# Probability rows of 16 or of 8 keys a head in the pooled attention of a two-layer kernel

## The chip, the cores and the metric

The kernel runs on one core of one Trainium2 chip. The metric is the device time of one execution in microseconds (us); the time before is the median of three runs, 1923.88 us (1922.08 to 1924.26). In what follows PE is TensorE, PEld its weight loads, DVE VectorE, ACT ScalarE, POOL GpSimd and SP SyncE; "L1619" is line 1619 of the kernel before.

## The reference

Two layers over 2048 tokens of width 512. The first is an RWKV recurrence beside a gated feed-forward of two experts. The second is attention over pooled keys beside a mixture of 16 routed experts (each token uses 4) and 2 shared ones. The change lies in the second layer's attention. There are 16 heads, 4 key groups, and at this length the first 1792 tokens are pooled in blocks of 64, so that they make 28 keys; the last 256 tokens are keys of their own:

```python
pool = lambda a: jnp.concatenate([a[:, :, :remote].reshape(Bq, HKV, nblk, MB, a.shape[-1]).mean(axis=3), a[:, :, remote:]], axis=2)
k_sem2, k_geo2, v2 = (pool(k_sem), pool(k_geo), pool(v))
k_pos = jnp.concatenate([jnp.arange(nblk) * MB + (MB - 1), jnp.arange(remote, Tq)])
...
scores = jnp.einsum('bhqd,bhkd->bhqk', q_sem, k_sem2) * (1.0 / jnp.sqrt(float(DS))) + jnp.einsum('bhqd,bhkd->bhqk', q_geo, k_geo2) * (1.0 / jnp.sqrt(float(DG)))
scores = scores * jnp.exp(logit_scale)[None, :, None, None]
mask = k_pos[None, :] <= pos[:, None]
scores = jnp.where(mask[None, None], scores, NEG_INF)
probs = jax.nn.softmax(scores, axis=-1)
out = jnp.einsum('bhqk,bhkd->bhqd', probs, v2)
out = out.transpose(0, 2, 1, 3).reshape(Bq, Tq, H * DV)
return out @ Wo
```

A key is seen by the queries at or behind its position. A tile of 128 tokens with number i therefore sees at most 2 (i + 1) pooled keys: 4 in tile 1, 8 in tile 3, 28 in tile 13. (Token tile 0 holds queries that see no key at all and gets a treatment of its own.)

## The kernel before

All work is in 32-bit floats. A scheduler places every instruction on its engine's queue by priorities and dependencies; the written order is only its starting point. Each engine then works through its queue in order.

The first layer takes the trace up to about 975 us. The second layer then makes the routing, keys and values (up to about 1200 us), the two last token tiles with their unpooled keys (`full_group`, L1443 to L1500), the shared experts (`hidden_shared`, `down_shared`, up to 1333 us), and then one long stage in which two things are interleaved by hand:

- **Row tiles.** Tokens were sorted by expert into tiles of 128 rows; 64 tiles always exist, up to 80 may, and 73 do here. Row tile j loads its rows (`x`, L1674) and its expert's weights (`w`, L674 to L678) on SP, turns the rows on PE (`tp`, L1681), multiplies (`ph`, L1688), and a tile later multiplies back (`py`, L1712). DVE scales the result into `y` (L1717, four buffers), and POOL adds its two halves into `comb` in memory by two indirect DMAs with addition (L1720). Each of them waits for the one before it in the same half. Tiles from number 65 on are under a condition, one branch each (L1737), and the scheduler moves nothing across these branches. Weights have three buffers, rows of x four.
- **Attention pieces.** After most of the first 64 row tiles one piece of `attention()` (L1630) is taken: the queries of two token tiles (`pq`, L1367; DVE's rotation by cos and sin, L1378 to L1383), the scores of one token tile (`scores`, L1571: `ps` on PE at L1576 and L1582, DVE's L1592 adds the mask and leaves the result in a buffer, then the softmax), or probabilities and values of one token tile (`turned` and `values`).

`turned` (L1598) brings a token tile's probabilities, kept as heads by keys, to keys on partitions: `pt` by transposes on PE (L1608), `sT` by a copy on ACT (L1613). `values` (L1616) multiplies each 128 rows of sT with the matching rows of values already multiplied by Wo (`pw`, L1619), and ACT copies the result into xT (L1623). How many of each a token tile needs follows from the room its probabilities stand in (`room_of`, L1564):

- tile 0: 32 keys a head, 512 columns: four transposes and four products;
- tiles 1 to 7: one of three buffers `near` of 16 keys a head, 256 columns: two and two. Only the first 2 (i + 1) keys of a head are written, and the rest was zeroed once at L1562;
- tiles 8 to 13: a buffer `wide` each, 32 keys a head: four and four.

The rows of values for 32 keys are `vo`; for 16 keys a copy in another order, `vo8`, is put together through memory: SP writes vo out (L1530) and reads it back in 16 pieces of 16 rows (L1531 to L1537). Tiles 0 to 4 go through `turned` and `values` inside the stage, tiles 5 to 13 (`LAST`) after its last row tile, while the last scatters into comb land. Then SP loads comb back (L1764), and ACT, DVE and SP finish and store the output (`close`, L1770 to L1780).

The xo loads (L1750) fetch, from row tile 48 on in the written order, what `close` adds at the end.

Of the kernel before, what the change touches and what calls it, by code (L numbers as in the profile page):

```python
# [9 lines left out]
F32 = mybir.dt.float32  # L10
# [7 lines left out]
P = 128  # L18
T = 2048
D = 512  # L20
# [24 lines left out]
H = 16  # L45
# [3 lines left out]
MB = 64  # L49
# [3 lines left out]
KP = 32  # L53
# [4 lines left out]
NARROW = 16  # L58
# [19 lines left out]
def tile_kernel(ctx: ExitStack, tc: tile.TileContext, a: dict):  # L78
    nc = tc.nc
# [4 lines left out]
    ident = const.tile([P, P], F32, name="ident")  # L84
# [30 lines left out]
    vo_d = dram.tile([P, HKV, D], F32, name="vo_d")  # L115
# [235 lines left out]
    for i in range(0, NT, 2):  # L351
        xin = n0.tile([P, 2, D], F32, tag="xin", bufs=NT // 2, name="xin")
        nc.sync.dma_start(
            out=xin, in_=a["x"][i * P : (i + 2) * P, :].rearrange("(n p) d -> p n d", p=P)
# [10 lines left out]
        out=wdc, in0=gate0_w[:, :, 1], in1=gate0_w[:, :, 0], op=ALU.subtract  # L365
    )
    wdp = n0ps.tile([P, NC, P], F32, tag="tp", name="wdp")
    for c in range(NC):
        dg = n0.tile([P, P], F32, tag="dg", bufs=2, name="dg")
        nc.vector.tensor_scalar(  # L370
            out=dg, in0=ident, scalar1=wdc[:, c : c + 1], scalar2=None, op0=ALU.mult
# [16 lines left out]
        out=upper, in_=upper, compare_op=ALU.is_gt, fill=0.0, base=0,  # L388
# [7 lines left out]
        out=eno, in0=col[:, 0:NST], scalar1=float(P), scalar2=None, op0=ALU.mult  # L396
# [4 lines left out]
    for i in range(0, NT, 2):  # L401
# [4 lines left out]
            out=shift, in0=mv[:, :, 0], scalar=-1.0, in1=rstd, op0=ALU.mult, op1=ALU.mult  # L406
        )
        for j in range(2):
# [6 lines left out]
                out=junk, in0=xn, in1=wdiff, scale=1.0, scalar=0.0, op0=ALU.mult, op1=ALU.add,  # L415
# [13 lines left out]
    for _ in range(2):  # L429
# [3 lines left out]
        out=sel[:, :, 0], in0=dl, scalar1=0.0, scalar2=None, op0=ALU.is_le  # L433
# [3 lines left out]
        out=sel[:, :, 1], in0=dl, scalar1=0.0, scalar2=None, op0=ALU.is_gt  # L437
# [3 lines left out]
        out=m, in0=dl, scalar=-1.0, in1=dl, op0=ALU.mult, op1=ALU.min  # L441
# [8 lines left out]
    for o, tri in ((0, upper), (N2, sums)):  # L450
        nc.tensor.matmul(
            out=tab[:, o : o + N2], lhsT=tri, rhs=sel.rearrange("p n e -> p (n e)"),
# [7 lines left out]
        out=run.rearrange("p e n -> p (e n)"), data0=newrow.rearrange("p e n -> p (e n)"),  # L460
# [8 lines left out]
        out=full, in0=own.to_broadcast([P, NT // 2]), in1=eno2[:, :, 1], op=ALU.is_gt  # L469
# [4 lines left out]
        out=paired[:, 0:1], in0=paired[:, 1:2], scalar1=2.0 * P, scalar2=None, op0=ALU.mult  # L474
    )
    nc.vector.tensor_tensor(
        out=pair_e[:, 0 : NSP - 1], in0=eno2[0:1, :, 0],
# [3 lines left out]
        out=pair_e[:, NSP - 1 : NSP], in0=own[0:1, :], in1=paired[0:1, 0:1], op=ALU.is_le  # L481
    )
    nc.vector.tensor_scalar(
        out=paired[:, 1:2], in0=paired[:, 0:1], scalar1=-1.0, scalar2=float(T),
# [4 lines left out]
        out=run[:, 1, :], in0=run[:, 1, :], scalar1=paired[:, 0:1], scalar2=None, op0=ALU.add  # L489
# [3 lines left out]
        out=row, in0=within, in1=run.rearrange("p e n -> p n e"), op=ALU.add  # L493
# [3 lines left out]
        out=alone, in0=row[:, :, 0], scalar1=paired[:, 0:1], scalar2=paired[:, 1:2],  # L497
# [10 lines left out]
        out=past, in0=bc(rowf, 2, C3), in1=bc(eno, 1, C3), op=ALU.is_ge  # L508
# [6 lines left out]
        out=place, in0=at, scalar=float(-P), in1=rowf, op0=ALU.mult, op1=ALU.add  # L515
    )
    nc.vector.tensor_tensor(
        out=past, in0=bc(at, 2, C3), in1=bc(col[:, 0:NST], 1, C3), op=ALU.is_equal
# [4 lines left out]
    for f in range(3):  # L523
        nc.vector.tensor_tensor(
            out=put[:, :, f, :], in0=past, in1=bc(facts[:, f, :], 2, C3), op=ALU.mult
# [3 lines left out]
    for i0 in range(0, NT, HN):  # L529
        if i0 == 2 * HN:  # L530
# [3 lines left out]
            out=hot, in0=bc(place[:, i0 : i0 + HN], 2, [P, HN, P]),  # L534
            in1=bc(col, 1, [P, HN, P]), op=ALU.is_equal,
        )
        for i in range(HN):
            nc.tensor.matmul(
                out=listed, lhsT=hot[:, i, :], rhs=put[:, i0 + i],
# [194 lines left out]
    for b in range(BEFORE):  # L734
# [14 lines left out]
    vo = ak.tile([P, HKV, D], F32, name="vo")  # L749
# [33 lines left out]
        out=m_pool, in_=m_pool, compare_op=ALU.is_ge, fill=0.0, base=1 - MB,  # L783
# [3 lines left out]
        out=n_pool, in_=n_pool, compare_op=ALU.is_ge, fill=MASKED, base=1 - MB,  # L787
# [15 lines left out]
    for t_ in n_full:  # L803
        own = t_[:, t_.shape[1] - P :]
        nc.gpsimd.affine_select(
            out=own, in_=own, compare_op=ALU.is_ge, fill=MASKED, base=0,
# [39 lines left out]
    for i in range(NT):  # L846
        yg = tr.tile([P, D], F32, tag="yg", bufs=6, name="yg")
        nc.gpsimd.indirect_dma_start(
            out=yg, out_offset=None, in_=ys0,
            in_offset=bass.IndirectOffsetOnAxis(ap=slot0[:, i : i + 1], axis=0),  # L850
        )
        g = acc[:, i, 0:D]
# [5 lines left out]
    for b in range(BEFORE, NRB):  # L858
        for i, po in carried(b):
            g = acc[:, i, 0:D]  # L860
# [3 lines left out]
    for b in range(NRB):  # L864
# [4 lines left out]
        for s in range(n):  # L869
            nc.vector.tensor_tensor(  # L870
                out=xr[:, s, :], in0=xr[:, s, :], in1=acc[:, i0 + s, 0:D], op=ALU.add
# [3 lines left out]
        for s in range(n):  # L875
            i = i0 + s
            nc.vector.tensor_scalar(
                out=acc[:, i, 0:D], in0=xr[:, s, :], scalar1=mv[:, s, 0:1],
# [3 lines left out]
        if (i + 1) % (TB // P) == 0:  # L882
            t0 = i + 1 - TB // P
            pl = m1y.tile([NR, TB], F32, tag="py", name="pl")
            for c in range(NC):
                nc.tensor.matmul(  # L886
                    out=pl, lhsT=cent[:, c, :], rhs=xT[:, c, t0 * P : (i + 1) * P],
# [10 lines left out]
    for b in range(NRB):  # L898
        rows2 = slice(b * RB, (b + 1) * RB)
        if b < PER:  # L900
            k0 = b * RB // MB
            nc.vector.tensor_reduce(
                out=xsum[:, :, k0 : k0 + RB // MB],
                in_=xT[:, :, rows2].rearrange("p c (n m) -> p c n m", m=MB),
                axis=AX.X, op=ALU.add,
            )
        else:
            nc.vector.tensor_reduce(
                out=xsum[:, :, NBLK : NBLK + 1],
                in_=xT[:, :, rows2].rearrange("p c (n m) -> p c n m", m=LW),  # L910
# [23 lines left out]
        out=upper, in_=upper, compare_op=ALU.is_gt, fill=0.0, base=0,  # L934
# [52 lines left out]
    with tc.tile_pool(name="rt", bufs=1, side="right") as rt, tc.tile_pool(  # L987
        name="rt2", bufs=2, side="right"
# [9 lines left out]
        for dst, tri in ((within, upper), (count, sums)):  # L998
            nc.tensor.matmul(
                out=dst.rearrange("p n e -> p (n e)"), lhsT=tri,  # L1000
# [6 lines left out]
            out=run.rearrange("p e n -> p (e n)"), data0=newrow.rearrange("p e n -> p (e n)"),  # L1007
# [5 lines left out]
            out=full, in0=run[:, :, NT - 1 : NT].to_broadcast([P, NR, NT]),  # L1013
# [6 lines left out]
            out=end, data0=sums[:, 0:NR], data1=ntl, initial=0.0, op0=ALU.mult, op1=ALU.add  # L1020
# [7 lines left out]
            out=run, in0=bc(first_tile, 2, [P, NR, NT]), scalar=float(P), in1=run,  # L1028
# [4 lines left out]
            out=row, in0=within, in1=run.rearrange("p e n -> p n e"), op=ALU.add  # L1033
# [3 lines left out]
        for k in range(KR):  # L1037
            one = rt2.tile([P, NT, NR], F32, tag="one", bufs=1, name="one")
            nc.vector.scalar_tensor_tensor(
                out=one, in0=rank, scalar=float(k + 1), in1=row, op0=ALU.is_equal, op1=ALU.mult,  # L1040
# [10 lines left out]
            out=acc[:, :, D : D + NR], in0=row, in1=bc(tot, 2, [P, NT, NR]), op=ALU.mult  # L1051
# [5 lines left out]
        for i in range(NT):  # L1057
            for k in range(KR):
                ins = nc.gpsimd.indirect_dma_start(  # L1059
                    out=xs,  # L1060
                    out_offset=bass.IndirectOffsetOnAxis(ap=slot[:, i, k : k + 1], axis=0),
                    in_=acc[:, i, :], in_offset=None,
# [21 lines left out]
        for m0 in (0, HM):  # L1084
# [4 lines left out]
                out=past, in0=bc(tno[:, ms], 2, sh3), in1=bc(end, 1, sh3), op=ALU.is_ge  # L1089
# [419 lines left out]

    sem = wq.tile([P, NC, H, KP], F32, name="sem")  # L1510

    vo8 = wq.tile([P, 2, D], F32, name="vo8")
    with tc.tile_pool(name="fold", bufs=1, side="right") as fold:
        wqs = fold.tile([P, NC, H * DH], F32, name="wqs")
        nc.sync.dma_start(out=wqs, in_=a["Wq_sem"])
# [12 lines left out]
                )  # L1528
            nc.scalar.copy(sem[:, :, 4 * g : 4 * g + 4, :], pa)
    nc.sync.dma_start(out=vo_d, in_=vo)  # L1530
    for p in range(2):  # L1531
        for u in range(2):
            for j in range(4):
                nc.sync.dma_start(
                    out=vo8[(4 * u + j) * NARROW : (4 * u + j + 1) * NARROW, p, :],
                    in_=vo_d[j * KP : j * KP + NARROW, 2 * p + u, :],
                )  # L1537

    down_shared(NTB - 1, hT)
    for tb in range(NTB - 1):  # L1540
# [17 lines left out]
    WIDE = NARROW * MB // P  # L1558
# [5 lines left out]
    def room_of(i):  # L1564

        if i == 0:
            return aq.tile([P, H, KP], F32, tag="t1", name="all_keys"), KP
        nk = (i + 1) * P // MB
        return (near[i % 3] if i < WIDE else wide[i - WIDE]), nk

    def scores(i, qg, u):  # L1571
        cols = slice(u * P, (u + 1) * P)
# [25 lines left out]
    def turned(i):  # L1598

        s = waiting.pop(i)  # L1600
        keys = s.shape[2]
        each = P // keys
        nw = H // each

        pool, tag = (m1y, "py") if i in LAST else (aps, "pa")
        pt = pool.tile([P, nw, P], F32, tag=tag, name="pt")
        for g in range(nw):
            nc.tensor.transpose(  # L1608
                pt[:, g, :], s[:, each * g : each * (g + 1), :].rearrange("p h k -> p (h k)"),
                ident,  # L1610
            )
        sT = aq2.tile([P, HKV, P], F32, tag="sT", name="sT")
        nc.scalar.copy(sT[:, 0:nw, :], pt)  # L1613
        return i, nw, sT, vo if keys == KP else vo8

    def values(i, nw, sT, by_row):  # L1616
        pw = aps.tile([P, NC, P], F32, tag="pa", name="pw")
# [274 lines left out]
```

## Time and profile before

| what | value |
|---|---|
| median of three runs | 1923.88 us (1922.08 to 1924.26) |
| the profiled execution | 1919.63 us |
| its span, first to last instruction | 1917.9 us |
| mean granted PE clock | 0.990 |
| PE busy over the span | 1848.1 us (96%) |
| PEld, DVE, ACT, POOL busy | 1286.8, 762.0, 536.5, 461.5 us |
| DMA | 381.40 MB, mean 199 GB/s |
| stage of row tiles | 1334 us to about 1876 us |
| transposes pt L1608 from near | 14, of which 6 before 1500 us |
| products pw L1619 | 84 records from 1330 us on, two for each product of 128x512 |

The table of windows gives, for a stretch of time, each engine's busy time, the granted clock in parts of one, and the mean busy share of the 16 DMA engines. The chain that ended last is followed back from the last instruction: each piece has its start, its length and what ran. A line of the timeline has start, length, engine, source line, operation, what it writes and reads, and in brackets how long the engine was idle before and what ended that.

### The profile page before, as it was taken

What the parts mean: (1) busy time and instruction counts of PE and PEld (TensorE: products, weight loads), DVE (VectorE), ACT (ScalarE), POOL (GpSimd) and SP (SyncE); (2) the same over time, 40 slices, a digit from 0 to 9 for tenths busy, and PEclk for the clock granted to TensorE, in tenths of its full rate; (3) what the DMA queues carried; (4) which work ended last, traced back from release to release, by engine and by line L of the source; (5) the groups of instructions that cost most, each with busy time, mean ns of one, the idle gap of its engine ahead of it and who ended that gap; (6) DMA issues with size and microseconds to landing.
All of it is one profiled execution on the core that took longest, in us unless ns stands there. A gap on an engine that the chain in (4) does not pass through costs nothing.

```text
span 1917.9 us, 23670 instructions
## 1 busy us (share of the span) xinstructions
PE 1848.1 (96%) x8107; PEld 1286.8 (67%) x8107; DVE 762.0 (40%) x1528; ACT 536.5 (28%) x1006; POOL 461.5 (24%) x349
## 2 busy tenths in 40 slices
PE   6999999999999999999989999999999999999996
PEld 4777777777877777777533654445767777777662
DVE  8354545272725435352166543421323223233313
ACT  6224232332423232332134112221222222222223
POOL 0211121120212111010210453000344444444341
PEclk9899999999999999999999999999999999999998
DMA  8657686635563434437461553122999999999896
GB/s 269 223 180 249 234 272 213 211 99 173 163 222 113 154 120 133 143 99 252 149 213 49 180 207 115 50 83 71 316 298 306 329 309 269 279 272 269 229 257 186
DMA packets 235989, 381.40 MB, mean 199 GB/s; under 512 B 19405, under 2 KB 136909, under 8 KB 234969
## 3 DMA queue, kind: packets, MB, share of 16 engines
q1 hardware_dynamic: 205784, 332.79, 52.3%
q0 software_dynamic: 28784, 45.63, 10.6%
q10 hardware_dynamic: 1296, 1.41, 0.3%
q8 instruction: 67, 1.10, 0.2%
q14 instruction: 58, 0.47, 0.1%
HBM read 294.04 MB, written 85.72 MB: 198 GB/s over the span
## 4 chain that ended last, share of the span: by engine, by line
PE 56%; DMA 6%; DVE 1%; issue 1%; ACT 1%; POOL 1%; SPq 0%; DVEq 0%; ACTq 0%; POOLq 0%
PE ph L1688 10%; PE py L1712 9%; PE pg L585 8%; PE py L607 4%; PE py L1121 4%; PE ph L972 3%; DMA comb<-y,to 3%; PE pq L1367 2%; PE proj L219 2%; PE po L727 2%; PE tp L1681 2%; PE ps L1576 1%; PE ps L1582 1%; PE pl L886 1%; PE pw L1492 1%
## 5 line engine op out<-in xcount | busy, mean ns | idle before, releaser
L585 PE MATMUL pg<-xg,w 128*128 128x256 f32 (+1 forms) x2304 | 494.9, 368 | 0.0
L585 PEld LDWEIGHTS pg<-xg,w 128*128 128x128 f32 x2304 | 419.5, 190 | 90.5 <-issue 42.3
L1720 POOL DMA_INDIRECT comb<-y,to x146 | 228.1, 1562 | 313.9 <-DMA comb<-y,to 183.4
L607 PE MATMUL py<-wd,hT 128*128 128x512 f32 x544 | 257.1, 593 | 3.5 <-DVE hT L592 3.5
L1688 PEld LDWEIGHTS ph<-xg,w 128*128 128x128 f32 (+1 forms) x1776 | 202.0, 182 | 40.4 <-ACT xg L1683 36.6
L1688 PE MATMUL ph<-xg,w 128*128 128x128 f32 (+1 forms) x1776 | 216.3, 278 | 0.7 <-issue 0.3
L592 DVE TENSOR_TENSOR hT<-sg,pg 128x256 f32<-128x256 f32 (+1 forms) x144 | 57.3, 402 | 380.4 <-ACT sg L590 380.2
L1712 PE MATMUL py<-w,ht 128*128 128x512 f32 (+1 forms) x438 | 207.8, 593 | 0.0
L590 ACT ACTIVATE sg<-pg 128x256 f32<-128x256 f32 (+1 forms) x144 | 53.0, 370 | 359.6 <-PE pg L585 359.3
L607 PEld LDWEIGHTS py<-wd,hT 128*128 128x128 f32 x544 | 102.2, 190 | 73.0 <-issue 61.9
L1717 DVE TENSOR_SCALAR y<-py,g 128x512 f32<-128x512 f32 x73 | 54.6, 748 | 219.7 <-PE py L1712 219.7
L958 ACT ACTIVATE ht<-ph,b1t 128x128 f32<-128x128 f32 (+1 forms) x222 | 81.2, 366 | 178.2 <-PE ph L1688 176.1
L1712 PEld LDWEIGHTS py<-w,ht 128*128 128x128 f32 (+1 forms) x438 | 75.9, 191 | 51.4 <-issue 45.2
L1683 ACT COPY xg<-tp 128x512 f32<-128x512 f32 x74 | 43.3, 585 | 186.9 <-PE tp L1681 186.9
L1121 PE MATMUL py<-w,hT 128*128 128x512 f32 (+1 forms) x192 | 89.4, 595 | 0.0
L972 PE MATMUL ph<-xT,w 128*128 128x512 f32 (+1 forms) x192 | 88.0, 597 | 0.0
L1059 POOL DMA_INDIRECT xs<-acc,slot x64 | 63.2, 987 | 66.0 <-DMA xs<-acc,slot 43.6
L267 POOL TENSOR_TENSOR ex<-st_p,qt 128x1024 f32<-128x1024 f32 x8 | 18.3, 2287 | 235.7 <-DVE qt L266 235.7
L727 PE MATMUL po<-wo,yb 128*128 128x512 f32 x128 | 57.4, 607 | 9.7 <-ACT acc L736 9.7
L1681 PEld LDWEIGHTS tp<-ident,x 128*128 128x128 f32 x296 | 36.9, 140 | 38.6 <-issue 20.8
L219 PE MATMUL proj<-xm,wr 128*128 128x256 f32 x256 | 61.5, 396 | 0.0
L219 PE MATMUL proj<-xm,wk 128*128 128x256 f32 x256 | 60.2, 389 | 0.0
(412 smaller groups left out, 2142.5 us busy)
## 6 DMA issues: line engine op xcount, KB each, us to landing
w<-in_w_dram SPq DMA_DIRECT2D x152, 352.0 KB
w<-in_w_dram SPq DMA_DIRECT2D x152, 256.0 KB
w<-in_w_gate_dram SPq DMA_DIRECT2D x72, 512.0 KB
w<-in_w_up_dram SPq DMA_DIRECT2D x72, 512.0 KB
wd<-in_w_down_dram SPq DMA_DIRECT2D x72, 512.0 KB
xs<-zero SPq DMA_DIRECT2D x16, 1360.0 KB
x<-xs SPq DMA_DIRECT2D x74, 272.0 KB
w<-in_w_dram SPq DMA_DIRECT2D x76, 192.0 KB
```

Of the source, the lines that this page charges most:

```text
L219: nc.tensor.matmul(out=ps[:, j, :], lhsT=w_[:, c, (o0 + j) * P : (o0 + j + 1) * P], rhs=xm[:, c, :], start=(c == 0), stop=(c == NC - 1),)
L585: nc.tensor.matmul(out=pg[:, i, 0:n], lhsT=w[:, c, i * FH + f * P : i * FH + (f + 1) * P], rhs=xg[:, c, 0:n], start=(c == 0), stop=(c == N ...
L607: nc.tensor.matmul(out=p, lhsT=hT[:, u * P : (u + 1) * P], rhs=wd[:, f, :], start=first_, stop=last_,)
L727: nc.tensor.matmul(out=po, lhsT=yb[:, c, s * P : (s + 1) * P], rhs=wo[:, c, :], start=(c == 0), stop=(c == NC - 1),)
L958: nc.scalar.activation(dst, src, AF.Relu, bias=b)
L972: nc.tensor.matmul(out=ph[0:n, :], lhsT=up(w, f, n, c), rhs=xT[:, c, cols], start=(c == 0), stop=(c == NC - 1),)
L1059: ins = nc.gpsimd.indirect_dma_start(out=xs, out_offset=bass.IndirectOffsetOnAxis(ap=slot[:, i, k : k + 1], axis=0), in_=acc[:, i, :], in_ ...
L1121: nc.tensor.matmul(out=py, lhsT=hT[0:n, e, f, s * P : (s + 1) * P], rhs=down(w, f, n), start=(e == 0 and f == 0), stop=(e == NS - 1 and f ...
L1681: nc.tensor.transpose(tp[:, c, :], x[:, c * P : (c + 1) * P], ident)
L1688: nc.tensor.matmul(out=ph[0:n, :], lhsT=up(w, f, n, c), rhs=xg[:, c, :], start=(c == 0), stop=(c == NC - 1),)
L1712: nc.tensor.matmul(out=py, lhsT=hT[0:n, f, :], rhs=down(w, f, n), start=(f == 0), stop=(f == NF1 - 1),)
L1720: nc.gpsimd.indirect_dma_start(out=c_, out_offset=bass.IndirectOffsetOnAxis(ap=to, axis=0), in_=y[:, h * D // 2 : (h + 1) * D // 2], in_of ...
```

## The change

The buffers near are used in two ways. A token tile that sees at most 8 keys (tiles 1, 2 and 3) takes the first 128 columns of its buffer as 16 heads by 8 keys, so that one transpose and one product of values do. Tiles 4 to 7 still take all 256 columns as heads by 16 keys; since a buffer's columns now hold leftovers of the other layout, POOL zeroes it before each of these four (a memset that was not there). There are two tables of rows of values now, one for 8 and one for 16 keys a head, each read back from memory in 16 pieces, of 8 and of 16 rows. `turned` finds out from the room how many columns there are. Which tiles are conditional and which come last is as before.

```diff
--- before.py
+++ after.py
@@ -1509,7 +1509,7 @@
 
     sem = wq.tile([P, NC, H, KP], F32, name="sem")
 
-    vo8 = wq.tile([P, 2, D], F32, name="vo8")
+    by_keys = {k: wq.tile([P, H * k // P, D], F32, name=f"vo{k}") for k in (8, 16)}
     with tc.tile_pool(name="fold", bufs=1, side="right") as fold:
         wqs = fold.tile([P, NC, H * DH], F32, name="wqs")
         nc.sync.dma_start(out=wqs, in_=a["Wq_sem"])
@@ -1528,13 +1528,18 @@
                 )
             nc.scalar.copy(sem[:, :, 4 * g : 4 * g + 4, :], pa)
     nc.sync.dma_start(out=vo_d, in_=vo)
-    for p in range(2):
-        for u in range(2):
-            for j in range(4):
+    for k, rows_ in by_keys.items():
+        for h in range(H):
+            r0 = h * k
+            while r0 < (h + 1) * k:
+                r1 = min((h + 1) * k, r0 // P * P + P)
+                k0 = h % 4 * KP + r0 - h * k
                 nc.sync.dma_start(
-                    out=vo8[(4 * u + j) * NARROW : (4 * u + j + 1) * NARROW, p, :],
-                    in_=vo_d[j * KP : j * KP + NARROW, 2 * p + u, :],
-                )
+                    out=rows_[r0 % P : r0 % P + r1 - r0, r0 // P, :],
+                    in_=vo_d[k0 : k0 + r1 - r0, h // 4, :],
+                )
+                r0 = r1
+    by_keys[KP] = vo
 
     down_shared(NTB - 1, hT)
     for tb in range(NTB - 1):
@@ -1566,7 +1571,16 @@
         if i == 0:
             return aq.tile([P, H, KP], F32, tag="t1", name="all_keys"), KP
         nk = (i + 1) * P // MB
-        return (near[i % 3] if i < WIDE else wide[i - WIDE]), nk
+        if i >= WIDE:
+            return wide[i - WIDE], nk
+        room = near[i % 3]
+        if nk <= 8:
+            return room.rearrange("p h k -> p (h k)")[:, 0 : H * 8].rearrange(
+                "p (h k) -> p h k", k=8
+            ), nk
+        if i * P // MB <= 8 + len(near) * P // MB:
+            nc.gpsimd.memset(room, 0.0)
+        return room, nk
 
     def scores(i, qg, u):
         cols = slice(u * P, (u + 1) * P)
@@ -1599,19 +1613,17 @@
 
         s = waiting.pop(i)
         keys = s.shape[2]
-        each = P // keys
-        nw = H // each
+        nw = H * keys // P
 
         pool, tag = (m1y, "py") if i in LAST else (aps, "pa")
         pt = pool.tile([P, nw, P], F32, tag=tag, name="pt")
         for g in range(nw):
             nc.tensor.transpose(
-                pt[:, g, :], s[:, each * g : each * (g + 1), :].rearrange("p h k -> p (h k)"),
-                ident,
+                pt[:, g, :], s.rearrange("p h k -> p (h k)")[:, g * P : (g + 1) * P], ident,
             )
         sT = aq2.tile([P, HKV, P], F32, tag="sT", name="sT")
         nc.scalar.copy(sT[:, 0:nw, :], pt)
-        return i, nw, sT, vo if keys == KP else vo8
+        return i, nw, sT, by_keys[keys]
 
     def values(i, nw, sT, by_row):
         pw = aps.tile([P, NC, P], F32, tag="pa", name="pw")
```

## The prediction

> **What bounds the kernel now.** I read the table of slices first, then the chain that ended last, then, for the stage that the change is in (1334 us to the end), the table of windows, PE's part of the chain, and DVE beside POOL.
>
> ```profile
> core 0: us, PE busy (x) PEld busy (x) DVE busy (x) ACT busy (x) POOL busy (x), PEclk, DMA share, GB/s
> 1400.00:1500.00 100.00, 99.85 (x571) 72.25 (x571) 25.72 (x90) 27.09 (x65) 43.42 (x28) 1.00 1.03 305
> 1700.00:1800.00 100.00, 99.97 (x546) 72.48 (x545) 33.10 (x99) 23.44 (x55) 41.35 (x27) 1.00 0.91 255
> 1800.00:1830.00 30.00, 30.00 (x158) 20.28 (x158) 8.90 (x27) 7.30 (x17) 9.88 (x7) 1.00 0.93 268
> 1830.00:1917.00 87.00, 65.41 (x290) 39.07 (x288) 25.10 (x42) 28.20 (x51) 24.68 (x16) 0.88 0.73 213
> ```
>
> PE has no gap between 1400 and 1830 at the full granted clock; but the 16 DMA engines are as full (share 1.03), so busy shares alone do not say which of the two paces the stage. The chain does. It is PE all the way here, one instruction behind the other, round an attention piece of token tile 1:
>
> ```profile
> 1412.83 0.44 PE tp L1681 x4
> 1413.27 0.22 PE pt L1608 x2
> 1413.49 0.86 PE py L1712 x2
> 1414.35 2.66 PE ph L1688 x24
> 1417.01 1.72 PE pw L1619 x4
> 1418.72 1.72 PE py L1712 x4
> 1420.44 0.44 PE tp L1681 x4
> 1420.88 0.86 PE py L1712 x2
> 1421.74 2.79 PE ph L1688 x24
> ```
>
> The two lines that the change halves, L1608 and L1619, stand on this chain with their whole length. The list of waits from 1340 to 1826 agrees: PE's side waits 32 us in 59 pieces for xg, and only 4.1 us in 17 for weights; SP, which issues the weights, waits 141.6 us for PE's py to free their buffers. So PE paces the loads.
>
> After the stage another bound takes over: the scatter-adds into comb, each of which waits for the landing of the one before in its half.
>
> ```profile
> 1805.41 0.74 DVE L1717 TENSOR_SCALAR y<-py,g 128x512 f32<-128x512 f32 x1
> 1860.34 0.75 DVE L1717 TENSOR_SCALAR y<-py,g 128x512 f32<-128x512 f32 x1 [4.52 <-PE py L1712]
> ```
>
> ```profile
> 1806.43 1.97 POOL L1720 DMA_INDIRECT comb<-y,to  x1 [6.81 <-DVE mx L1348]
> 1873.40 1.55 POOL L1720 DMA_INDIRECT comb<-y,to  x1 [0.75 <-DMA comb<-y,to]
> ```
>
> Row tile 62's y is ready at 1806.15 and its scatter starts 0.28 us later: up to there POOL has no arrears. Row tile 72's y is ready at 1861.09 and its scatter starts 12.3 us later: PE runs 5.8 us a tile without attention pieces, the scatters 7.3 us a tile, and the last scatters set the end. What PE saves before 1806 therefore moves the start of that last chain and is kept; what it saved after 1811 would be lost.
>
> **The change part by part.**
>
> PE's work. Token tiles 1, 2 and 3 (4, 6 and 8 keys) lose one transpose and one product each; the built program's order has three L1608 and three L1619 fewer, and all else on PE, DVE and ACT in its old order. All three products stand at 1417, 1487 and 1501 us, well before 1806. A product is half of 1.72 us: 0.86, three are 2.58. A transpose is half of 0.22: 0.11, three are 0.33 at most. But a pt piece also covers the wait for xg: the ph group behind it is 2.66 us with a pt ahead and 2.79 without, so 0.13 of cover shrinks to 0.11 and some 0.02 us each comes back. I take 3 x 0.09 = 0.27, between 0 and 0.33. Sum on the path: **2.85 us**, bounds 2.58 and 2.91.
>
> The Trainium skill (Perfetto Trace Analysis, section Identifying the Most-Contended Engine) says that matmul busy share is no good measure of PE and points to LDWEIGHTS busy share; here that is 0.72 beside 1.00. Read as a share of real work it would keep some 0.72 x 2.85 = 2.1 us, an estimate by that page; the chain above, where each L1619 instruction takes its 0.43 us from the next, speaks for the whole.
>
> ACT and DVE. ACT's copy of sT shrinks from 128x256 (0.38 us) to 128x128 (0.27, the row of L1470); ACT is busy a quarter of the time, so 0. DVE's rows for 8 keys only change their layout: 0.
>
> POOL. Four memsets of 128x256, before tiles 4 to 7; the row of L1562 gives 0.30 us each. They sit in POOL's queue behind the scatters of row tiles 8, 18, 20 and 29 and wait for the transposes of tiles 1 to 4. The scatters queue behind them, and DVE's addition L1592 of tiles 4 to 7 waits for them. In the trace of before the fourth is the tightest: its scatters leave POOL at 1561.06, tile 4's transposes end at 1562.68, the next scatter's y comes at 1562.81, and DVE needs the memset at 1625.79. The others are as loose, for POOL idles 2 to 6 us between pairs, waiting for landings. Cost 0; were POOL full, 4 x 0.30 = 1.2.
>
> SP. Ahead of the stage, L1534 issues 32 small loads for 16.
>
> ```profile
> 1271.25 10.23 SPq L1534 DMA_DIRECT2D vo<-vo_d  x16
> 1281.58 6.07 SPq L1129 DMA_DIRECT2D comb<-y  x4
> 1287.69 0.45 SPq L1358 DMA_DIRECT2D cs<-in_cos_dram  x1
> 1288.19 0.45 SPq L1359 DMA_DIRECT2D sn<-in_sin_dram  x1
> 1292.01 42.02 SPq L1129 DMA_DIRECT2D comb<-y  x10
> ```
>
> At 0.64 us each the added 16 take 10.2 us, to 1291.8. Behind them wait the comb writes of three y tiles (three buffers) and cs, sn. DVE writes the next y only at 1317.05, and cs is first read at 1336.03: 25 us of cover. Cost 0; without cover up to 10.2.
>
> In the stage SP's order moves. The cos load of block 2 goes ahead four row tiles and now waits for DVE's last read of block 1 (L1378, done 1448.75); SP comes there at about 1445, and the weight load behind it waited for PE until 1449.77 anyway. Five x loads go back one row tile, but x lands about 3 us after issue and x27, for one, had 24.8 us between its issue and its transposes; 16.8 or more stay. The xo loads, 512 KB each, go back two to five tiles; nobody reads them before 1895. All 0. The last stage's own work is unchanged.
>
> The sum is made against the profiled execution, 1919.63 us (span 1917.9): 1916.8. The median shown, 1923.88, is 4.25 above that execution; I carry the same difference over: 1923.88 - 2.85 = **1921.0 us**, 0.15% faster. About 0.2% (3.85 us) is what a measurement of this kernel can tell from no change, so the likeliest answer lies inside it.
>
> **The rivals.**
>
> *Nothing is gained.* The stage is paced by DMA after all. For it: share 1.03 and 305 GB/s from 1400 to 1500; POOL waits 169 us for comb landings from 1340 to 1826. Against it: PE has no idle time on weights, and the scatter lag falls back to 0.3 us on every second tile up to 62. Time 1923.9, chance 0.15.
>
> *The last chain gains more than PE.* A pair of scatters takes 7.3 us beside weight loads and 4.6 after the loads have ended (1855 us). If the shift lets one more pair of the nine run after the loads, another 2.7 us goes: 1918.3. For it: the last four pairs did run at 4.6 to 4.7; against it: loads and scatters are shifted by the same PE. Chance 0.15. The mirror of it, one pair fewer, ends at 1923.7 and belongs to the first rival's time.
>
> *Slower: the vo loads hold SP.* Place: L1534, 32 loads ahead of the comb writes. Price: if a load of 8 rows takes as long as a whole landing, as x<-xs does at 1334.35 (2.68 us on the chain, say 3 with its issue), the added 16 take 48 us; SP is late for DVE's y at 1317.05 by 48 - 35.5 = 12.5 us, py's two banks fill and PE stands: 1921.0 + 12.5 = 1933.5. It decides from 35.5 / 16 = 2.2 us a load. For it: all have the same source and each waits for a queue's earlier load. Against it: the 16 loads of before kept 0.64 us apart, and half the rows should not be slower. Chance 0.08. [...]
>
> *The change doesn't do what it says* is excluded by the built order: the six PE instructions are gone.
>
> **How the numbers follow.** Forecast 0.62, no gain 0.15, more 0.15, slower 0.08. Around each time lies some 1.5 us, as the three runs of before (1922.08 to 1924.26) spread. Faster by over 0.2% (under 1920.0) takes all of the "more" case and the lower edge of the forecast: 0.27. Slower by over 0.2% (over 1927.7) is the last rival and little else: 0.09. Between them 0.64. The range takes in the "more" case and no gain, with a spread: 1917.5 to 1925.0.
>
> **What would show it.** L1619 from 1400 to 1510 with 2 records in place of 4 for tiles 1 to 3, and the ph group after the pt at 2.66 to 2.79. Row tile 62's scatter some 2.9 us earlier, with a lag below 1 us; if its lag has grown by what PE saved, the first rival holds. L1534 with 32 issues in about 20 us and DVE's y near 1317 unchanged; later means the third rival. The memsets (line 1582 of the changed kernel) with no wait of DVE behind them. Row tiles 63 to 72 in about the same 58 us; shorter means the second rival. I would be wrong by a step that I hold at nothing: a scatter queue that falls behind earlier because of the memsets, or an x load that comes too late.

## The result, and the profile after

| | before | after |
|---|---|---|
| median of 20 runs each, us | 1920.56 (1917.81 to 1924.26) | 1918.66 (1915.40 to 1921.61) |
| ratio, 95% interval | | 0.9984 (0.9978 to 0.9990) |
| profiled execution, us | 1919.63 | 1916.60 |
| its span, us | 1917.9 | 1914.9 |

By the ratio the changed kernel is faster by 0.16%, that is 3.07 us of 1920.56, with an interval from 1.9 to 4.2 us. The two medians in the table are 1.90 us apart, which is the lower end of it. It is a small gain, but 20 runs of each kernel tell it from none.

The same two windows of the table of stages as before, of the changed kernel (first to last column: window, its length, busy time of PE, PE's weight loads, DVE, ACT and POOL, granted clock, DMA share, GB/s):

```profile
1400.00:1500.00 100.00, 99.85 (x573) 72.15 (x572) 25.69 (x90) 27.73 (x68) 44.42 (x31) 1.00 1.05 305
1830.00:1917.00 87.00, 62.15 (x268) 36.50 (x266) 23.88 (x37) 27.27 (x49) 21.71 (x14) 0.86 0.69 199
```

The stage looks as it did: PE without a gap, and the DMA engines as full. The three records of POOL that are new between 1400 and 1500 are memsets. Where the time went is seen only in the instructions. PE's timeline of the changed kernel, round the attention piece of token tile 1:

```profile
1412.69 0.27 PE L1621 MATMUL pt<-ident,near 128*128 128x128 f32 x1
1412.80 1.02 PE L1724 MATMUL py<-w,ht 128*128 128x512 f32 x2
1413.66 2.85 PE L1700 MATMUL ph<-xg,w 128*128 128x128 f32 x24
1416.34 1.02 PE L1631 MATMUL pw<-vo,sT 128*128 128x512 f32 x2
1417.20 1.88 PE L1724 MATMUL py<-w,ht 128*128 128x512 f32 x4
```

A group's length on this view ends with the modelled end of its last matmul, so the starts are the better measure: from pt to py 0.11 us where the chain of before had 0.22, from pw to py 0.86 where it had 1.72. The ph group behind the pt takes 2.68 us, 0.02 more than before (2.66); the other groups shown have kept their length.

The step is best followed in DVE's y of each row tile (line 1717 before, 1729 after). I subtract its time before from its time after. The difference is -0.42 us from row tile 3 to 9, -1.35 at row tile 10 (the values of token tile 1 lie before it), -2.30 at 20 (tile 2), -3.24 at 22 (tile 3), and between -3.0 and -3.2 from there to row tile 72. Three steps of 0.93, 0.95 and 0.94 make **2.82 us**. The first -0.42 is not the change: by row tile 0, executions of the kernels here lie between 0.2 us and 4.2 us later than the profiled execution of before, whatever their edit, and all but one (the last experiment below) lose about 0.6 us of that by row tile 3; why is not known. So below, times are counted from the y of row tile 3 (1365.46 us before, 1365.04 us after), which lies ahead of the transposes and products that the edits change in the stage. (The run with late values also puts other attention pieces between the first row tiles; its y of row tile 3 has lost the same 0.6 us.)

DVE's y of row tile 62 and 72, and POOL's first scatter of each, after:

```profile
1802.32 0.74 DVE L1729 TENSOR_SCALAR y<-py,g 128x512 f32<-128x512 f32 x1
...
1857.11 0.75 DVE L1729 TENSOR_SCALAR y<-py,g 128x512 f32<-128x512 f32 x1 [4.52 <-PE py L1724]
```

```profile
1803.34 1.97 POOL L1732 DMA_INDIRECT comb<-y,to  x1 [6.81 <-DVE mx L1348]
...
1868.71 1.55 POOL L1732 DMA_INDIRECT comb<-y,to  x1 [0.36 <-issue]
```

Row tile 62's scatter comes 3.09 us earlier, and its lag (from the end of y to the start of the scatter) is 0.28 us as before. Row tile 72's comes 4.69 us earlier: the last scatters gained 1.5 us on their own. The end of the span gained 3.0. So what the scatters won did not arrive, and that was the first sign that they don't set the end.

SP's and POOL's side work, after:

```profile
1271.44 16.02 SPq L1537 DMA_DIRECT2D vo<-vo_d  x32
```

```profile
1413.09 0.32 POOL L1582 MEMSET near<- 128x256 f32 x1 [0.94 <-PE pt L1621]
...
1483.57 0.91 POOL L1582 MEMSET near<- 128x256 f32 x1
```

The 32 small loads take 0.50 us each in the mean: those of 8 rows start 0.34 us apart, those of 16 rows 0.46, and once SP stands still for some 3 us, as it does in the kernel before. One memset, which POOL had waited for, took 0.32 us, the other three, behind a scatter, about 0.9.

### The profile page after: what moved, and what is told of

The parts are those of the page before. It is cut to its first block, busy times and chain, and to the rows that moved or that the text cites. A ratio compares the mean times of both kernels' runs of the same rounds, so it can differ in the third digit from the quotient of the medians.

```text
span 1914.9 us, 23683 instructions
## 1 busy us (share of the span) xinstructions
PE 1844.1 (96%) x8098; PEld 1283.4 (67%) x8098; DVE 761.8 (40%) x1528; ACT 536.9 (28%) x1006; POOL 462.5 (24%) x353
```

## The experiments

The theory at the start was **PE**: the stage is paced by PE, each token tile with half the values saves 0.95 us, and it is kept. The rivals were **order** (the moved loads and the new rooms make the gain), **DMA** (transfers pace the stage) and **side cost** (memsets and vo loads take back a part). The first four runs are for these. The ratios are to the kernel before, each with its 95% interval.

**One token tile alone.**

```diff
-        if nk <= 8:
+        if nk <= 4:
```

> Only token tile 1 keeps 8 keys a head; tiles 2 and 3 go back to 16. All side work of the change stays (32 small loads, memsets before tiles 4 to 7, and two more before 2 and 3). Theory PE (each of the three token tiles takes 0.94 us off PE's unbroken chain, and that is the gain): 0.94 us from the PE chain, so about -0.9 us against the kernel before (ratio 0.9995), plus at most the 0.5 us that the trace of the change gained on the first row tiles for another reason. In the trace, y of row tiles 10 to 60 some 0.9 to 1.4 us earlier than before, in one step. Rival order (the new order of SP's queue gives the gain, the PE work is covered): the same -3 us as the change (ratio 0.9984). Rival DMA (loads pace the stage): 0.

Measured: 0.9996 (0.9987 to 1.0005). DVE's y makes one step, of 0.94 us, at row tile 10, and none at 20 and 22. The interval alone would not tell this from nothing; the step does. The lags of the scatters between row tiles 18 and 32 rose to as much as 9 us in this run and were gone by row tile 62 (0.28 us), without any loss of y.

**The side work alone.**

```diff
-        if nk <= 8:
-            return room.rearrange("p h k -> p (h k)")[:, 0 : H * 8].rearrange(
-                "p (h k) -> p h k", k=8
-            ), nk
-        if i * P // MB <= 8 + len(near) * P // MB:
+        if 8 <= i * P // MB <= 8 + len(near) * P // MB:
```

> The change without its saving: both tables of values are loaded in 32 pieces and POOL zeroes the buffers before tiles 4 to 7, but tiles 1 to 3 keep 16 keys a head, two transposes and two products. Theory PE: the side work is hidden, so 0 against the kernel before within 0.5 us (ratio 0.9998 to 1.0003), no step in y of the row tiles. Rival order: a gain stays, -1 to -3 us. Rival side cost (the memsets and loads cost something that PE's saving of more than 3 us pays for): +0.5 to +1.5 us, seen as y late by that much after row tile 30.

Measured: 1.0002 (0.9993 to 1.0011), with no step at row tiles 10, 20 and 22. The y of row tiles 36 to 66 is 0.13 us late against that of row tile 3, and this is gone at row tile 67. So the table of 8 keys with its loads, the memsets and the moved loads bring nothing like the three steps, and what they cost in the stage does not reach its end. The rivals order and side cost fall.

**Eight keys without memsets.**

```diff
-        room = near[i % 3]
         if nk <= 8:
-            return room.rearrange("p h k -> p (h k)")[:, 0 : H * 8].rearrange(
+            t = aq.tile([P, H, KP], F32, tag=f"t{2 - i % 2 if i > 1 else 2}", name="few")
+            return t.rearrange("p h k -> p (h k)")[:, 0 : H * 8].rearrange(
                 "p (h k) -> p h k", k=8
-            ), nk
-        if i * P // MB <= 8 + len(near) * P // MB:
-            nc.gpsimd.memset(room, 0.0)
-        return room, nk
+            ), 8
+        return near[i % 3], nk
```

> The change without its four memsets inside the stage: tiles 1 to 3 score all 8 keys, the masked ones get probability 0, and their 128 columns stand in the scratch tiles of the queries, so the near buffers stay clean. PE, DVE and ACT do a little more for tiles 1 and 2 (128 columns for 64 and 96; on PE these are at the shortest spacing already). Theory PE: the memsets cost nothing, so the same as the change, -3 us against before (ratio 0.9984, within 0.5 us). Rival side cost: 0.5 to 1.5 us better than the change, ratio 0.9977 to 0.9981. In the trace the lag of the scatters behind y at row tiles 18 to 32, 3.5 to 6.5 us in the change, goes back to the 2 to 4 us of before if the memsets made it.

Measured: 0.9992 (0.9981 to 1.0003). Three steps of 0.94 us, and 2.88 us in all by row tile 72, so the gain is there without the memsets; the time is above the expected 0.9984, but this lies inside the interval. The lags of the scatters of row tiles 18 to 32 are 3.7 to 6.8 us here too, so the memsets are not what raised them in the changed kernel.

**The kernel before with the work doubled.** The transposes and products of tiles 1 to 3 are issued twice into the same place.

```diff
-        for g in range(nw):
+        twice = 2 if 1 <= i <= 3 else 1
+        for g in (*range(nw),) * twice:
```

> The kernel before with the transposes and the products of tiles 1 to 3 done twice over (the second round writes the same again): 6 transposes and 6 products more on PE, no other work. Theory PE: 6 x (0.86 + 0.11) = +5.8 us, twice what the change removes with the other sign; ratio 1.0030. y of the row tiles late in three steps of 1.9 us. Rival DMA (the stage is paced by loads and scatters that have arrears): less than half of it, +0 to +2.5 us, with PE's idle time shrinking instead.

Measured: 1.0036 (1.0022 to 1.0050). Steps of 1.94, 1.94 and 1.93 us, in all 5.81. The price of a transpose with its product is 0.97 us where it is added, and 0.94 where the change takes it out. DMA as the pace of the stage falls: it could have hidden a loss or a gain, and hid neither.

The next runs were to carry the theory further, with the second half of the prediction's picture: that **scatters** set the end behind the stage.

**The values of tiles 1 to 4 behind the last row tile.**

```diff
-    near = [aq.tile([P, H, NARROW], F32, name=f"near{i}") for i in range(3)]
+    near = [
+        aq.tile([P, H, 8 if i < 4 else NARROW], F32, name=f"near{i}") for i in range(1, WIDE)
+    ]
...
-    LAST = range(5, FULL[0])
+    LAST = range(1, FULL[0])
```

> The changed kernel, with a room of its own for each of token tiles 1 to 7 (no memsets inside the stage) and with the transposes and products of tiles 1 to 4 moved behind the last row tile, where PE waits for the scatters anyway; the last pair's xo is loaded after the stage to make room. Nothing is left out. Theory PE (PE alone paces the stage up to row tile 62): the stage loses a further 3 x 0.97 us for tiles 1 to 3 and 1.94 us for tile 4, 4.85 us against the changed kernel and 7.7 us against the kernel before: ratio 0.9960, row tile 62's scatter some 7.7 us earlier than before, still with a lag under 1 us. Rival scatters (a pair of scatters takes 7.3 us beside the loads, 73 pairs fill the stage of 533 us, so that the scatter chain has no room left): the scatter of row tile 62 lags by the 4.85 us, the end does not move against the changed kernel: ratio 0.9984. Between them: part of it, with the lag that grows by the rest.

Measured: 0.9983 (0.9974 to 0.9992), nothing more than the change. That is the number of the rival, but not its mechanism. Against row tile 3, the y of row tile 62 came 7.5 us earlier than before, as theory PE said, with a lag of 0.28 us: the scatters did follow. Then the gain was gone at the end. Neither theory held.

**Less of PE's work from row tile 64 on, alone.**

```diff
-            for c in range(NC):
+            cs_ = NC - 1 if j >= 64 else NC
+            for c in range(cs_):
```

> The changed kernel, with work left out for the last row tiles alone: from row tile 64 on, the up projection sums over three of its four blocks, 3 matmuls of 12 less in each of nine row tiles, about 9 x 0.33 = 2.9 us of PE. Theory PE until row tile 62, scatters after it: the y tiles come up to 2.9 us earlier, the lags of their scatters grow by the same, the end stays: 0.9984 against the kernel before, as the changed kernel. Rival all PE work counts alike: 2.9 us more, 0.9969.

Measured: 0.9959 (0.9945 to 0.9972), where no gain over 0.9984 was expected. (I had mis-sized the edit: a row tile's ph shrank from 2.76 to 2.19 us, not by 0.33, and there are ten of them with the spare one, 5.7 us, so that "all PE work counts" gives 0.9984 - 0.0030 = 0.9954.) Work after 1811 us is on the path. That overturns the theory of the end, and the last 60 us of the traces show what sets it. Of before, ACT's and DVE's timelines at the closing:

```profile
1892.28 0.58 ACT L1623 COPY xT<-pw 128x512 f32<-128x512 f32 x1 [2.79 <-PE pw L1619]
1892.88 1.28 ACT L1772 ACT_TABLE_LOAD   x1
1894.18 2.00 ACT L1772 ACTIVATE y<-y 128x1024 f32<-128x1024 f32 x2
```

```profile
1895.27 2.36 DVE L1774 TENSOR_TENSOR y<-xT,y 128x1024 f32<-128x1024 f32 x2 [34.17 <-DMA y<-comb]
```

The same two views of the changed kernel:

```profile
1888.94 0.59 ACT L1635 COPY xT<-pw 128x512 f32<-128x512 f32 x1 [2.79 <-PE pw L1631]
1889.54 1.28 ACT L1784 ACT_TABLE_LOAD   x1
1890.84 2.00 ACT L1784 ACTIVATE y<-y 128x1024 f32<-128x1024 f32 x2
```

```profile
1891.92 2.36 DVE L1786 TENSOR_TENSOR y<-xT,y 128x1024 f32<-128x1024 f32 x2 [34.07 <-ACT y L1784]
```

ACT takes its work in order. The first close stands behind the copy of token tile 11's values, and that copy waits for PE. From the end of that copy to DVE's first closing instruction it is 2.40 us, before and after and in all the other kernels here: table load, one activation, no wait for the loads from comb. DVE then runs 16 instructions without a gap, and the span ends 22.6 and 23.0 us after its first. So PE's tail, the values of token tiles 5 to 13, sets the end, not the scatters. The label "DMA y<-comb" in DVE's line of before names the wrong one of two releasers (ACT's first activation ends at 1895.24 us, 0.03 us ahead of DVE's start), and the chain misled me in the same way. The chain of the changed kernel:

```profile
1883.04 6.45 DMA y<-comb
...
1889.50 5.26 DMA y<-comb
...
1895.34 1.22 DVE y L1790
```

It reaches 1895.34 through two landings. But DVE had been busy without a gap since 1891.92; the instruction at 1895.34 waited for its engine. A chain that jumps onto an engine in the middle of an unbroken row of work has taken a landing that was merely close in time.

PE's timeline of the changed kernel from the last row tile on:

```profile
1856.93 2.92 PE L1700 MATMUL ph<-xg,w 128*128 128x128 f32 x24
1864.14 1.08 PE L1621 MATMUL pt<-ident,near 128*128 128x128 f32 x4 [4.29 <-PEq L1749]
1865.27 3.78 PE L1631 MATMUL pw<-vo,sT 128*128 128x512 f32 x4
...
1873.68 3.60 PE L1631 MATMUL pw<-vo,sT 128*128 128x512 f32 x8
```

This ph group belongs to no row tile: 73 exist, and the loop is one ahead. After it PE idles 4.29 us while seven conditions are skipped (PEq L1749). The mean granted clock is 0.58 from 1862 to 1866 and 0.57 from 1866 to 1870, and the first four records of pw take 3.57 us to the next start, against 1.72 at the full clock. These idle and slow stretches are what made the tail look like waiting. They don't free it: nothing else is late.

The experiment with the late values is now explained: 4.85 us of PE's work went from the stage into the tail, on the same path. Token tile 11's copy ends 0.11 us later than in the changed kernel.

**Closing additions on POOL, alone and with the late values.**

```diff
-        nc.vector.tensor_tensor(out=y, in0=y, in1=rest_of[i], op=ALU.add)
+        add = nc.gpsimd if i in (2, 6, 10) else nc.vector
+        add.tensor_tensor(out=y, in0=y, in1=rest_of[i], op=ALU.add)
```

> The changed kernel, with the closing addition of xo of pairs 2, 6 and 10 on POOL in place of DVE. Theory: the closing is paced by DVE, 16 instructions one every 1.14 us from 1891.9 to 1910.1; with three of them on POOL (2.3 to 3.2 us each there, beside DVE) DVE ends 3.4 us earlier, unless ACT's or the comb loads' landing is then late: 1 to 3.4 us off, ratio 0.9966 to 0.998. Rival: DVE is slowed by POOL beside it, or the loads from comb set the closing and not DVE: no change or slower against the changed kernel, 0.9984 or more.

> Both of the last edits that leave nothing out: the values of tiles 1 to 4 behind the last row tile, and three closing additions on POOL. Theories PE and DVE both right: 7.7 us and 1 to 3.4 us off the kernel before, ratio 0.9942 to 0.9955. If the scatters set the stage, only the second: 0.9966 to 0.998.

Measured: 1.0003 (0.9994 to 1.0012) for both, some 3.6 us slower than the changed kernel. For the second that lies outside all that was expected. The rival of the first holds: DVE is slowed by POOL beside it. DVE's and POOL's timelines of the first of the two kernels:

```profile
1896.19 2.36 DVE L1786 TENSOR_TENSOR y<-xT,y 128x1024 f32<-128x1024 f32 x2 [34.29 <-ACT y L1784]
...
1899.61 4.51 DVE L1786 TENSOR_TENSOR y<-xT,y 128x1024 f32<-128x1024 f32 x2
```

```profile
1898.70 3.20 POOL L1791 TENSOR_TENSOR y<-y,xo 128x1024 f32<-128x1024 f32 x1 [19.74 <-DMA y<-comb]
```

Two of DVE's products take 4.51 us beside POOL's addition and 2.36 without it. Each of the three additions saves DVE 1.14 us and costs it 2.15. That the closing is paced by DVE is borne out all the same: the loss arrives in full.

**24 keys for token tiles 8 to 11.** This is the change taken a step further, and the first test made for the new theory.

```diff
-    by_keys = {k: wq.tile([P, H * k // P, D], F32, name=f"vo{k}") for k in (8, 16)}
+    by_keys = {k: wq.tile([P, H * k // P, D], F32, name=f"vo{k}") for k in (8, 16, 24)}
...
-    wide = [aq.tile([P, H, KP], F32, name=f"wide{i}") for i in range(WIDE, FULL[0])]
+    wide = [
+        aq.tile([P, H, 24 if i < 12 else KP], F32, name=f"wide{i}") for i in range(WIDE, FULL[0])
+    ]
```

> The changed kernel, with its edit taken one step further: token tiles 8 to 11, which see 18 to 24 pooled keys, keep heads by 24 keys, 3 transposes and 3 products in place of 4; some 18 more small vo loads ahead of the stage, about 9 us by the 0.50 us of the changed kernel's, under the cover that the first 16 left; the last pair's xo is loaded after the stage to make room. Nothing is left out. Their values all stand in PE's tail behind the last row tile. Theory PE to the end (the tail's copy of token tile 11 lets ACT start the closing, and DVE follows without a gap): 4 x 0.97 = 3.9 us against the changed kernel, ratio 0.9964, as long as the loads from comb are there in time. Theory scatters set the end, as predicted: PE's tail is beside the path, 0.9984.

Measured: 0.9969 (0.9959 to 0.9979), a median of 1913.22 us. Against row tile 3, token tile 11's copy ends 4.10 us earlier than in the changed kernel (expected 3.9), although the loads from comb begin 0.69 us later. It is faster than both kernels: its interval lies below 0.9984 and overlaps that of the changed kernel (0.9978 to 0.9990) by 0.0001 alone, and the trace has the 4.1 us beside it.

**Fewer scatters, and more.** Two kernels, with one edit each.

```diff
-        for h, c_ in enumerate(comb):
+        for h, c_ in enumerate(comb[0:1] if j >= 68 else comb):
```

```diff
-        for h, c_ in enumerate(comb):
+        for h, c_ in list(enumerate(comb)) * (2 if j == 70 else 1):
```

> The changed kernel without the second half's scatter (into the second half of comb) of row tiles 68 to 72: five scatters of the last ten left out. The loads from comb then start some 8 to 15 us earlier. Theory PE to the end: nothing changes at the end, 0.9984. Theory scatters set the end: at least 5 us off, 0.996 or less.

> The changed kernel with the two scatters of row tile 70 done twice (its rows are added twice). The chain of scatters and the loads from comb behind it come one pair later, 4.6 to 7.3 us. Theory PE to the end: in the changed kernel the first pair's loads are there about 5.6 us before ACT takes them (by e6, where ACT took them 5.8 us after SP's issue), so that 0 to 1.7 us of it is seen: 0.9984 to 0.9993. Theory scatters set the end: all of it, 1.0008 to 1.0022.

Measured: 0.9990 (0.9981 to 1.0000) and 0.9989 (0.9980 to 0.9997). The first told less than it was meant to: each scatter that is left still waits for its y and for the landing before it, so the loads from comb began only 1.8 us earlier, not 8 to 15. The second is clear: they began 6.18 us later, and the closing by 0.5 us in the profile. ACT's timeline of the second shows how near that came to the limit:

```profile
1892.89 1.06 ACT L1784 ACTIVATE y<-y 128x1024 f32<-128x1024 f32 x1
1894.11 1.06 ACT L1784 ACTIVATE y<-y 128x1024 f32<-128x1024 f32 x1 [0.16 <-DMA y<-comb]
```

Only here does ACT wait for a load from comb, 0.16 us. So the scatters have some 5.5 us of slack in the changed kernel: 6.18 less this wait and less the 0.5 us by which ACT itself came later.

**24 keys, without the row tile that does not exist.**

```diff
-            made = hidden_rows(j) if j < NRT else None
+            made = None
+            if FULL_TILES < j < NRT:
+                with tc.If(held > j):
+                    made = hidden_rows(j)
+            elif j < NRT:
+                made = hidden_rows(j)
```

> The kernel with 24 keys (the run before this one), without a piece of work that no output needs: at the first row tile that does not exist, the loop of before and after still loads a row tile and runs its 4 transposes and 24 up projections, 0.44 + 2.76 = 3.2 us of PE between the last row tile and the tail. Here the hidden part of a conditional row tile stands in a condition of its own inside the first, one condition more for each of eight row tiles. Theory PE to the end: 3.2 us less than with 24 keys alone, 0.9969 - 0.0017 = 0.9952, if the inner conditions cost PE nothing; a skipped condition costs up to 4.3 / 7 = 0.6 us now, and eight executed ones at most the same each would take 4.9 us, which ends at 0.9978. Theory scatters set the end: 0.9969 still, or more.

Measured: 0.9983 (0.9974 to 0.9992), a little past the outer bound that was given (0.9978), which lies inside the interval. It is slower than with 24 keys alone by the trace; the two intervals overlap (0.9974 to 0.9979). PE's timeline shows the price:

```profile
1817.01 0.60 PE L1695 MATMUL tp<-ident,x 128*128 128x128 f32 x4
1818.34 2.92 PE L1702 MATMUL ph<-xg,w 128*128 128x128 f32 x24 [0.73 <-ACT xg L1697]
```

Inside a condition of its own the hidden part can't be mixed with the down part of the row tile before, and PE waits 0.73 us for ACT's xg in each of eight row tiles: the pace goes from 5.81 to 6.67 us. But it settles the dispute better than a gain would have. The scatters keep up at this pace, so the loads from comb begin 2.98 us *earlier* than with 24 keys alone, and token tile 11's copy ends 2.82 us *later*. The time goes with the copy.

The kernels from the late values on against the changed kernel, in us from the y of row tile 3 (a minus is earlier):

| kernel | SP's first load from comb | end of tile 11's copy | DVE's first closing | ratio to before |
|---|---|---|---|---|
| before | +3.76 | +2.91 | +2.93 | 1 |
| after | 0 | 0 | 0 | 0.9984 |
| values of 1 to 4 late | -2.10 | +0.11 | +0.11 | 0.9983 |
| less PE after row tile 64 | -0.67 | -6.26 | -6.25 | 0.9959 |
| additions on POOL | +2.32 | +0.23 | +0.23 | 1.0003 |
| late values and POOL | -4.30 | -0.98 | -0.97 | 1.0003 |
| 24 keys | +0.69 | -4.10 | -4.09 | 0.9969 |
| fewer scatters | -1.82 | -0.94 | -0.92 | 0.9990 |
| more scatters | +6.18 | +0.48 | +0.49 | 0.9989 |
| 24 keys, no spare row tile | -2.29 | -1.28 | -1.26 | 0.9983 |

DVE's start follows the copy to 0.03 us in every row, and the scatters in none. (With additions on POOL the ratio also holds what DVE lost behind its start.)

Two rows move by 0.5 to 0.9 us although their edits leave PE's work as it is, fewer and more scatters. This is PE's own: their last ph group starts within 0.02 us of the changed kernel's, and behind it PE idles 4.03 and 5.17 us at the skipped conditions where it idled 4.29, and its clock is at half for 3.4 and 6.8 us where it was for 6.8. So the 0.5 us of the kernel with more scatters is not the scatters' either. With less PE work it idled 3.55 us, which is most of why that copy moved by 6.26 us for the 5.7 us taken out. What sets these two lengths is not shown; one execution of each kernel is profiled.

## Why the prediction was right or wrong

**PE's price: right.** The term was 2.85 us, and the three steps measure 2.82. Doubling the same work cost 5.81 us for six transposes and products, 0.97 each, against 0.94 for each that the change takes out. Most of the difference is the cover that was to come back, 0.02 us a transpose: the ph group behind the pt takes 2.68 us by the starts where it took 2.66, at each of the three token tiles. The Trainium skill's measure (Perfetto Trace Analysis, section Identifying the Most-Contended Engine), from which I worked out an estimate of 2.1 us by the weight loads' share of 0.72, is below each of these sums; here the steps in y decide for the whole.

**Side work at nothing: right, with two sizes off.** The 16 added vo loads took SP's queue 5.8 us longer (16.02 against 10.23) instead of 10.2: the 0.64 us each that the prediction took from before had SP's one stop in it. Three of the four memsets took 0.9 us instead of 0.30. Both were covered, as the run with the side work alone shows, and DVE's y of 1317.05 came at 1317.23.

**DMA as no bound: right, with one reading too wide.** The prediction says of before that the scatter lag falls back to 0.3 us on every second tile up to 62. It does so, to 0.3 to 0.5 us, from row tile 39 on; from 9 to 38 it lies between 0.6 and 4.8 us. That argument against the first rival therefore covered only the later part of the stage; the run with doubled work and the steps in y settle it for the whole.

**The end of the kernel: wrong, without a price here.** The step "After the stage another bound takes over: the scatter-adds into comb" and its conclusion, that what PE saved after 1811 would be lost, failed. The path stays on PE to the copy of token tile 11, and goes by ACT and DVE to the end. The lag of 12.3 us at row tile 72 was real, but I didn't ask who waits for it: in the changed kernel the loads from comb were some 5.5 us early. The change's three products lie ahead of 1806, where both pictures keep the saving, so the sum came out right for a reason that was half wrong, and that was luck. It is also why "the last chain gains more than PE" could not pay: the scatters did gain 1.5 us more than PE, and the end didn't.

**What a measurement can tell: wrong, and this decided the forecast.** "About 0.2% (3.85 us) is what a measurement of this kernel can tell from no change, so the likeliest answer lies inside it" is the step that failed. The prediction gives no working for this bound; all it had was three runs, 2.2 us apart. Twenty runs of each kernel give an interval of 0.06% to either side, and my own term of 0.15% lies clear of nothing by such a measure. With the mechanism as it was worked out, and 0.15 for no gain, faster should have been the likeliest answer. What came out, 0.16% by the ratio, agrees with the term; the steps in y, 2.82 us, show it without this noise.

**The time itself.** 1921.0 was 1923.88 less 2.85. Three runs had put before at 1923.88; twenty put it at 1920.56, and less 2.85 that is 1917.7, against 1918.66 measured. The base was off by more than the term.

## What to carry to other kernels

A lag on a queue is no bound until somebody waits for it: follow the end back from the last engine that runs without a gap, and look which instruction opened that row, before you call a long chain of landings the path. Where one engine is on the path from the stage to the end, moving its work along that path brings nothing, and only removing it counts, each instruction by its spacing on the timeline (here 0.94 to 0.97 us for a transpose and a product). Work out how finely the number of runs resolves a change before you call a small, sure gain no change.

## What the runs showed of the hardware that was not expected

- While PE had no work behind the last row tile, its granted clock fell to 0.5, in the changed kernel 2.8 us after the end of the last ph (1859.85 us), and stayed there for 6.8 us, into PE's next work: four records of pw took 3.57 us instead of 1.72 (1865.27 to 1868.84 us). In four of the fourteen traces the stretch lasts 3.4 us. Whether keeping PE busy in that gap would avoid it was not tried.
- An elementwise addition on POOL beside DVE's made two of DVE's products take 4.51 us instead of 2.36, and took 3.20 us itself.
- A memset of 128x256 on POOL took 0.30 to 0.32 us where POOL had waited ahead of it, and 0.89 to 0.91 where it followed a scatter's issue directly: all twelve in the changed kernel, the one with a single tile and the one with the side work alone (from 1400 us on) fall so. The longer record begins 0.98 us after the scatter's, inside that record of 1.55. Three that came later behind a scatter (1.09 to 1.45 us after its start, in later kernels) took 0.42 to 0.79 us, and like the others they end some 1.9 us after the scatter's start: the longer ones are partly the scatter's own.
- The lag of the scatters between row tiles 18 and 32 varies from trace to trace, between 0.3 and 9 us, with nothing lost by it; what sets it stays open.
